# Block 0 of a latent-attention kernel: rotary scores as scaled fp16 pairs, first products in halves of tokens, values three tiles behind, loads and stores issued by SP

## The chip, the cores and the metric

The kernel runs on one core of a Trainium2 chip. The metric is the device time of one execution in microseconds, the median of several runs. A profile of one execution is read beside it: it lists the instructions of each engine (TensorE or PE with its weight loads PEld, VectorE or DVE, ScalarE or ACT, GpSimd or POOL, SyncE or SP), their waits, and the TensorE clock that was granted.

## The reference

One layer over 2048 tokens of width 512: attention with compressed queries and keys, 16 heads, a residual and a layer norm, then one linear layer with a second residual and norm.

```python
cq = rms_norm(hidden_states @ w_qa.T, q_a_ln_w)                  # 384 wide
q = (cq @ w_qb.T).reshape(b, s, H, DQ).transpose(0, 2, 1, 3)     # 128 + 64 a head
q_nope, q_pe = (q[..., :DN], q[..., DN:])
q_pe = q_pe * cos + rotate_half(q_pe) * sin
ckv = hidden_states @ w_kva.T                                    # 128 + 64
k_pe = ckv[..., KVLR:].reshape(b, s, 1, DR).transpose(0, 2, 1, 3)
k_pe = k_pe * cos + rotate_half(k_pe) * sin
ckv_l = rms_norm(ckv[..., :KVLR], kv_a_ln_w)
kv = (ckv_l @ w_kvb.T).reshape(b, s, H, DN + DV).transpose(0, 2, 1, 3)
...
scores = jnp.einsum('bhqd,bhkd->bhqk', q_full, k_full) * scale   # causal, softmax
out = jnp.einsum('bhqk,bhkd->bhqd', attn, v)
...
x = _layernorm(x + attention(x)); x = _layernorm(x + ffn(x))
```

Everything is fp32 to the reader. The kernel keeps close to fp32 by splitting most operands into a high and a low part and adding three products (high by high, high by low, low by high).

## The kernel before, in words

The 2048 tokens are four query blocks of 512 (b = 0 to 3), each block has eight pairs of heads (p) and each pair four tiles of 128 queries (qt). `units` runs over p and qt of one block. A tile of block 0 needs at most 512 keys, so both heads of a pair share one PSUM tile (`pair_scores`, L598): scores, row maximum, exponential, sums. `pair_probs` (L619) scales and splits the probabilities into two fp16 parts `hl` on ScalarE and VectorE, and SP transposes them into `PT` by DMA. `values` (L630) multiplies them with the latent keys `V`, ScalarE copies the result to `ot`, and a DMA stores it to `ot_d`. `run_values(lag)` keeps the values `lag` tiles behind the scores: 2 in block 0, up to 3 later. After block 0 all values but one tile are finished before its memory is given back.

What a score needs is made in several places:

- `project_x(hb)` (L273) takes 256 tokens: it splits x into fp32r parts (ScalarE high, VectorE low), makes the key products (`ps_kv` or `ps_x`) and the query products (`ps_cq` or `ps_x`), the inverse norms on POOL (`rsqrt`), and turns queries and keys by TensorE transposes into `cq`, `Kn` (non-rotary keys), `Kp0` (rotary keys of block 0, in fp32r, scaled by `ku`) and `Kr` (all rotary keys, unscaled). Halves 0 and 1 belong to block 0 and run first.
- `weights_q(g)` (L196) multiplies the query weights of four heads with their key weights, sums their squares for a scale (`column_total`, `root`), and splits them into fp16 pairs `wq` and `wpe`, stored to DRAM.
- `late_keys` (L372) makes the rotary keys of blocks 1 to 3 (`Kp`, fp16 pairs) once all of `Kr` is there.
- `project_pe(b, g)` (L425) makes the rotary queries of four heads: two product groups of 512 tokens, four VectorE products with cosine and sine, an add and a subtraction (POOL; VectorE for the first group), then the stack `pe`: for each of four heads the high part on partitions 0 to 63, and the low part, value less `ph`, on 64 to 127. In block 0 the high copies are ScalarE's (L462) and the low subtractions VectorE's (L465, some on POOL for the first group), in fp32r; in blocks 1 to 3 both are POOL's, in fp16.
- `project_nope(b, p)` (L471) makes the non-rotary queries `qn` of a pair as fp16 pairs.

`score` (L500) adds five products for a head: three of `qn` with `Kn`, two of the stacked `pe` with the two parts of the rotary keys. In block 0 the last two are fp32r products, for which the width is at least 256 columns (L43, L600), even in tile 0 with its 128 keys.

Halves 2 to 7 of x and the weights of groups 1 to 3 are made inside block 0: `side` holds two generators, and `units` takes steps of them after each tile (L769 to L773); `fill` takes steps of the next pair's projections.

In block 0 and before it the order of instructions on each engine is the planner's, from a simulated timeline. From block 1 on TensorE and SP keep the order of the program text. Loads of raw x, of the cosine tables for keys and of raw weights are issued on ScalarE's queue; loads of `wq`, `wpe`, `cq` and the stores of `ot` on POOL's; SP issues the first loads, the transposes and the stores of `cq`, `wq` and `wpe`.

## Time and profile before

| | |
|---|---|
| median of 3 runs | 1573.07 us (1572.97 to 1578.87) |
| the profiled execution | 1576.4 us, span 1574.5 us |
| granted TensorE clock, mean | 0.981 |
| TensorE busy | 1497.7 us, 95% |
| VectorE, ScalarE, POOL busy | 1175.2, 945.6, 364.1 us |
| first scores of block 1 | 278.5 us after the span's start |
| last scores | 1310 us after it |

A row of the timeline or of the groups names the line of the code, the operation, what is written and what is read, and the shape. `[6.28 <-DVE pe L465]` after a row is idle time of that engine just before it and what ended it. A helper that issues for several callers has one line (L74 and L75 are the fp32r split, L68 and L69 the fp16 split). TensorE rows of products that follow one another overlap; the distance between two starts is the cost of one.

### The profile page before, as it was taken

How to read it: one execution, taken by the hardware profiler on the slowest of the kernel's cores; microseconds unless marked ns; L12 is line 12 of the kernel's file. 1: busy time of each engine (PE TensorE's matmuls, PEld its weight loads, DVE VectorE, ACT ScalarE, POOL GpSimd, SP SyncE). 2: the span in 40 equal slices, each digit the busy share in tenths (PEclk: the TensorE clock that was granted, in tenths of full speed). 3: DMA queues.
4: the chain of work that ended last, by engine and by line, in shares of the span. 5: the costliest groups of instructions: out<-in, count | busy, mean ns of one | idle time of the engine just before them, and what ended most of it. 6: DMA issues, size and time to landing. Idle time of an engine off the chain costs nothing. (4 is left out here: it accounts for less than half of the span.)

```text
span 1574.5 us, 24464 instructions
## 1 busy us (share of the span) xinstructions
PE 1497.7 (95%) x9062; PEld 1007.2 (64%) x9062; DVE 1175.2 (75%) x2140; ACT 945.6 (60%) x1701; POOL 364.1 (23%) x441
## 2 busy tenths in 40 slices
PE   7799996999999999999999999999999999999997
PEld 5477764566665566666666566566566666788886
DVE  6687877788888988888887777777777775465554
ACT  5687777566666676767775665666666665311220
POOL 2232342422405504040032400400400000022132
PEclk9899998999999999999999999999999999999999
DMA  5367556587898788888896788677678898433230
GB/s 208 114 138 188 128 121 143 118 163 149 161 180 173 146 161 157 162 154 160 155 197 127 153 151 162 133 142 160 132 148 164 160 230 207 138 121 120 94 114 34
DMA packets 611142, 234.94 MB, mean 149 GB/s; under 512 B 569712, under 2 KB 589296, under 8 KB 610384
## 3 DMA queue, kind: packets, MB, share of 16 engines
q1 hardware_dynamic: 601152, 212.38, 64.0%
q0 software_dynamic: 3200, 11.44, 2.4%
q10 hardware_dynamic: 6672, 9.57, 2.1%
q8 instruction: 71, 1.16, 0.3%
q14 instruction: 47, 0.39, 0.1%
HBM read 62.72 MB, written 28.05 MB: 58 GB/s over the span
## 5 line engine op out<-in xcount | busy, mean ns | idle before, releaser
L513 PE MATMUL s<-Kn,qn 128*128 128x512 f16 (+4 forms) x1920 | 471.7, 351 | 22.4 <-ACT pr L565 17.3
L565 ACT ACTIVATE pr<-s,bias,er 128x1024 f32<-128x1024 f32 (+3 forms) x320 | 324.3, 1016 | 212.3 <-DVE bias L559 160.1
L589 DVE SCALAR_TENSOR_TENSOR hl<-pr,inv,hl 128x1024 f16<-128x1024 f32 (+7 forms) x320 | 353.5, 1118 | 42.7 <-ACT hl L586 38.0
L641 PEld LDWEIGHTS <-V 128*128 128x128 f16 x3264 | 318.6, 98 | 89.0 <-DMA PT<-hl 9.9
L641 PE MATMUL o<-ring,V 128*128 128x256 f16 x3024 | 361.5, 273 | 1.2 <-DMA ring<-hl 1.2
L513 PE MATMUL s<-Kp,pe 128*128 128x512 f16 (+6 forms) x1280 | 353.7, 358 | 7.2 <-DVE pe L465 7.2
L586 ACT ACTIVATE hl<-pr,inv 128x1024 f16<-128x1024 f32 (+7 forms) x320 | 294.2, 960 | 80.3 <-ACT pr L565 34.5
L550 DVE TENSOR_REDUCE neg<-s 128x1 f32<-128x1024 f32 (+3 forms) x320 | 317.3, 992 | 18.2 <-PE s L513 14.7
L513 PEld LDWEIGHTS <-qn 128*128 128x128 f16 x1920 | 185.8, 98 | 175.2 <-issue 36.2
L513 PEld LDWEIGHTS <-pe 128*128 128x128 f16 x1152 | 112.9, 98 | 103.4 <-issue 0.7
L482 PE MATMUL ps_qn<-cq,wq 128*128 128x512 f16 x576 | 141.5, 393 | 7.8 <-ACT ot L646 4.9
L872 PE MATMUL acc<-wvo,oh 128*128 128x512 f32 x448 | 144.4, 403 | 2.0 <-ACT pr L565 2.0
L465 POOL TENSOR_TENSOR pe<-prod,ph 32x512 f16<-32x512 f32 (+1 forms) x92 | 127.2, 1383 | 16.2 <-issue 10.3
L449 POOL TENSOR_TENSOR prod<-prod 128x512 f32<-128x512 f32 x15 | 19.1, 1275 | 467.1 <-DVE prod L442 467.1
L482 PEld LDWEIGHTS <-wq 128*128 128x128 f16 x576 | 57.8, 101 | 73.3 <-issue 15.9
L577 DVE TENSOR_SCALAR inv<-sums 128x1 f32<-128x1 f32 x128 | 27.0, 211 | 99.8 <-ACT pr L565 99.3
L872 PEld LDWEIGHTS acc<-wvo,oh 128*128 128x128 f32 x448 | 83.4, 189 | 23.3 <-issue 4.4
L872 PE MATMUL acc<-wvo,ol 128*128 128x512 f32 x224 | 87.8, 392 | 0.0
L646 ACT ACTIVATE ot<-o 128x256 f32<-128x256 f32 x128 | 48.3, 378 | 38.6 <-PE o L641 29.7
L74 ACT ACTIVATE oh<-o 128x1024 fp32r<-128x1024 f32 x28 | 29.7, 1060 | 64.9 <-PE acc L872 49.3
L464 POOL CAST pe<-prod 32x512 f16<-32x512 f32 x88 | 67.1, 763 | 3.3
L75 DVE TENSOR_TENSOR ol<-o,oh 128x1024 fp32r<-128x1024 f32 x28 | 38.9, 1390 | 38.4 <-ACT oh L74 38.4
(198 smaller groups left out, 1684.2 us busy)
## 6 DMA issues: line engine op xcount, KB each, us to landing
o<-ot_d SPq DMA_DIRECT2D x32, 512.0 KB, 3.6
ot_d<-ot SPq DMA_DIRECT2D x97, 128.0 KB, 2.4
wq<-wq_d SPq DMA_DIRECT2D x22, 384.0 KB, 3.5
wo<-in_wo_dram SPq DMA_DIRECT2D x4, 1024.0 KB, 5.7
x<-in_x_dram SPq DMA_DIRECT2D x16, 256.0 KB, 3.7
out_dram<-xb SPq DMA_DIRECT2D x16, 256.0 KB, 2.0
ot_d<-ot POOLq DMA_DIRECT2D x31, 128.0 KB, 3.4
wpe<-wpe_d SPq DMA_DIRECT2D x10, 384.0 KB, 3.8
```

The costliest lines, as they stand in the source:

```text
L75: nc.vector.tensor_tensor(l, ps, h.bitcast(F32), ALU.subtract)
L464: nc.gpsimd.tensor_copy(to, rp[q, x, :])
L465: (nc.gpsimd if not quick or (b, g) == (0, 0) and j % 2 else nc.vector).tensor_tensor(pe[64 + 32 * x : 96 + 32 * x, j, :], rp[q, x, :], ph ...
L482: nc.tensor.matmul(ps, w[:, i, lt, j * P : (j + 1) * P], cq[:, k, lt, :], start=n == 0, stop=n == 8)
L513: nc.tensor.matmul(ps[:, :w], lhs, K[:, i, c0 : c0 + w], start=n == 0, stop=n == 4)
L550: nc.vector.tensor_reduce(neg[:, ti : ti + 1], v, axis=AX.XY, op=ALU.max, negate=True)
L565: nc.scalar.activation(pr[:, c0 : c0 + n * w].rearrange("p (a c) -> p a c", a=n), v, AF.Exp, bias=bias, scale=r, accum_out=sums[:, ti : ti ...
L586: nc.scalar.activation(hl[:, 0, c], pr[:, c], AF.Copy, scale=inv)
L589: nc.vector.scalar_tensor_tensor(hl[:, 1, c], pr[:, c], inv, hl[:, 0, c], ALU.mult, ALU.subtract)
L641: nc.tensor.matmul(ps[:, :256], vt[:, i, k % 4, :], v[:, :, l, k, :], start=n == 0, stop=n == 3 * kts - 1)
L646: nc.scalar.activation(ot, ps[:, :256], AF.Copy)
L872: nc.tensor.matmul(acc, l[:, t, c], state["wvo"][p][:, i, j, :], start=p == 0 and j == 0 and n == 0, stop=p == NPAIR - 1 and j == 1 and n ...
```

## The change

Block 0's rotary keys `Kp0` become fp16 pairs. They are scaled by a factor from the squares of the rotary keys of the first 512 tokens (`key_scales(0, 4)`), where before they were fp32r pairs scaled by `ku`. The rotary queries of block 0 become fp16 pairs too, scaled by `up[0]`. Low parts are now made in one difference over all four heads (`rope_split`), and the high and low parts are then copied to their places (`rope_stack`): in block 0 the high parts by POOL and the low parts by VectorE, in the first group of block 1 both by VectorE, later both by POOL. Scores are as wide as the keys, 128 columns in tile 0.

The first products of block 0 are written out in a fixed TensorE order: keys and queries of 256 tokens, weights of group 0, keys and queries of the second 256, then rotary and non-rotary products of 256 tokens at a time, then three steps of the weights of group 1. A PSUM pool `x` of four banks serves this stage. The products of weight group 0 stay in PSUM.

In `project_x` the low part of x, the scaled `nq` and the scaled `nk` are POOL's instead of VectorE's; x is split one step ahead; a call takes two steps instead of five. The loads of x, tables and weights, and block 0's loads of `wq`, `wpe`, `cq` and its stores of `ot` are issued by SP; a store is issued after the next tile's transpose. `wq` has two buffers. Values run three tiles behind, and the last two tiles of block 0 keep their `PT` in spare room of `qn` and `pe` and are finished in block 1. Score buffers `pr` and `hl` are shared by tiles of the same parity.

```diff
-        return [[(0, max(nk, 256))]]
+        return [[(0, nk)]]
...
-    Kp0 = blk0.tile([P, 2, QB], F32R, name="Kp0")
+    Kp0 = blk0.tile([P, 2, QB], F16, name="Kp0")
...
-    def late_scales():
+    def key_scales(i, n):
...
-        nc.vector.scalar_tensor_tensor(z, fk, K_UP, kvn, ALU.mult, ALU.add)
+        nc.vector.scalar_tensor_tensor(zs[i], fk, K_UP, kvn, ALU.mult, ALU.add)
...
+        nc.vector.tensor_scalar(up[i], rz, fk, K_UP / W_TOP, ALU.mult, ALU.mult)
...
+    def raw_weights(g):
+
+        wk = pa.tile([P, 4, P], F32, tag="wk", name=f"wk{g}")
+        nc.sync.dma_start(wk, a["wk"][:, 4 * g : 4 * g + 4])
+        raws = []
+        for lt in range(LT):
+            raws.append(pa2.tile([P, 4, P], F32, tag="wqb", name=f"wqb{g}_{lt}", bufs=3))
+            nc.sync.dma_start(raws[lt], a["wqb"][g, :, lt])
+        return wk, raws
...
+    def raw_x(hb):
+
+        raws = []
+        for kt in range(0, KT, 2):
+            raws.append(pa2.tile([P, 2, 256], F32, tag="xr", name=f"xr{hb}_{kt}", bufs=2))
+            nc.sync.dma_start(raws[-1], a["xT"][hb, :, kt : kt + 2])
+        csk = pa.tile([P, 2, 2, 64], F32, tag="csk", name=f"csk{hb}", bufs=2)
+        nc.sync.dma_start(csk, a["csk"][hb])
+        return raws, csk
...
+            pin(nc.scalar.activation(h, raws[n], AF.Copy))
+            pin(eng.tensor_tensor(l, raws[n], h.bitcast(F32), ALU.subtract))
...
+        if hb < 2:
+            split16(kf, Kp0[:, 0, cols], Kp0[:, 1, cols], ks[0])
...
+            nc.gpsimd.tensor_scalar(nq, nq, rk[:, 1:2], None, ALU.mult)
...
-    state = {"queue": nc.gpsimd}
+    state = {"queue": nc.sync}
...
+    def rope_split(b, prod, ph, cols, adds, low):
+
+        rp, tp = prod[:, 0, :, cols], prod[:, 1, :, cols]
+        adds[0].tensor_tensor(rp[:, 0, :], rp[:, 0, :], rp[:, 1, :], ALU.subtract)
+        adds[1].tensor_tensor(rp[:, 1, :], tp[:, 0, :], tp[:, 1, :], ALU.add)
+        h, l = ph[:, 0, :, cols], ph[:, 1, :, cols]
+        if b:
+            nc.scalar.activation(h, rp, AF.Copy)
+            low.tensor_tensor(l, rp, h, ALU.subtract)
+        else:
+            nc.scalar.activation(h, rp, AF.Copy, scale=up[0])
+            low.scalar_tensor_tensor(l, rp, up[0], h, ALU.mult, ALU.subtract)
+
+    def rope_stack(pe, ph, cols, js, engs):
+
+        for j in js:
+            q = slice(32 * j, 32 * j + 32)
+            for i in range(2):
+                for x in range(2):
+                    r = 64 * i + 32 * x
+                    engs[i].tensor_copy(pe[r : r + 32, j, cols], ph[q, i, x, cols])
...
-        for j in range(4):
-            q = slice(32 * j, 32 * j + 32)
-            for x in range(2):
-                to = pe[32 * x : 32 * x + 32, j, :]
-                if quick:
-                    nc.scalar.activation(to, rp[q, x, :], AF.Copy)
-                else:
-                    nc.gpsimd.tensor_copy(to, rp[q, x, :])
-                (nc.gpsimd if not quick or (b, g) == (0, 0) and j % 2 else nc.vector).tensor_tensor(
-                    pe[64 + 32 * x : 96 + 32 * x, j, :], rp[q, x, :], ph[q, x, :] if b else ph[q, x, :].bitcast(F32), ALU.subtract
-                )
+        rope_split(b, prod, ph, every, (nc.gpsimd, nc.gpsimd), nc.gpsimd if b else nc.vector)
+        pe = blk.tile([P, 8 if (b, g) == (0, 3) else 4, QB], F16, tag="pe", name=f"pe{b}_{g}")
+        if b == 0:
+            engs = (nc.gpsimd, nc.vector)
+        else:
+            engs = (nc.vector, nc.vector) if (b, g) == (1, 0) else (nc.gpsimd, nc.gpsimd)
+        rope_stack(pe, ph, every, range(4), engs)
...
+        put_in()
         yield
...
+    with tc.manual_schedule(engines={ET.PE}):
...
+        keys(0)
+        nqs = queries(0)
+        x.append(split_x(1, [x_r[1][:, kt : kt + 2] for kt in (0, 2)], nc.gpsimd))
+        w0 = weights_q(0, (*wq0, wpe0, wk0, wqb_r, wpe_r))
+        next(w0)
+        keys(1)
+        turn_queries(0, nqs, "x")
+        next(w0)
+        key_scales(0, 4)
+        exp_scale(0, slice(0, 1))
+        nqs = queries(1)
+        next(w0)
+        for hb in range(2):
+            turn_k(hb, flip[hb], "x")
...
+        for hb in range(2):
+            k = "xm"[hb]
+            cols = slice(hb * 256, hb * 256 + 256)
+            for i in range(2):
+                ps = psum[k].tile([P, 512], F32, tag=k, name=f"ps_pe0_0_{i}_{hb}")
+                rope_products(wpe0, state["cq"], state["cs"], prod, ps[:, :256], i, cols)
+            rope_split(0, prod, ph, cols, (nc.vector, nc.gpsimd), nc.vector)
+            rope_stack(pe, ph, cols, range(2), (nc.gpsimd, nc.vector))
+            if hb == 0:
+                turn_queries(1, nqs, "m")
+            for j in range(2):
+                ps = psum[k].tile([P, 512], F32, tag=k, name=f"ps_qn0_0_{j}_{hb}")
+                nope_products(wq0[0], state["cq"], qn, ps[:, :256], j, cols, kvq[0])
+            rope_stack(pe, ph, cols, range(2, 4), (nc.gpsimd, nc.vector))
+            if hb == 0:
+                for _ in w0:
+                    pass
+        next_x(2)
+        state["wq", 0, 1] = wq0[1]
+        w1 = weights_q(1)
+        for _ in range(LT):
+            next(w1)
...
-        lag = min(ring.shape[1] // (2048 * (b + 1)) - 1, 3) if b else 2
+        lag = min(ring.shape[1] // (2048 * (b + 1)) - 1, 3) if b else 3
...
+                    fill()
                     pi = pair_scores(pool, b, p, qt, nk)
                     flush()
                     probs.append(pair_probs(pool, b, p, qt, nk, PT, *pi))
-                    fill()
-                    next(side[0], None)
+                    if qt != 1:
+                        next(side[0], None)
                     if p < 5:
                         next(side[1], None)
-                    if qt % 2:
-                        next(side[0], None)
+                    if p + qt == 0:
+                        next(side[1], None)
                     run_values(lag)
                     run_values(lag)
...
-    while len(vals) > 1:
+    while len(vals) > 2:
         half_values()
```

## The prediction

> **What bounds the kernel now.** The page's busy times come first, with the granted TensorE clock over forty slices.
>
> ```profile
> PE 1497.7 (95%) x9062; PEld 1007.2 (64%) x9062; DVE 1175.2 (75%) x2140; ACT 945.6 (60%) x1701; POOL 364.1 (23%) x441
> ...
> PEclk9899998999999999999999999999999999999999
> ```
>
> TensorE is busy for 95% of the span, so only its 77 us of idle time and its slow stretches can be won. Both lie at the left end. The windows view, cut where the stages change, says how much (after the name of each stretch: its length, and per engine the busy us; near the end the granted clock).
>
> ```profile
> 0.00:12.70 12.70, 8.75 (x36) 5.24 (x36) 5.69 (x19) 5.97 (x12) 2.56 (x9) 1.00 0.80 267
> 12.70:61.20 48.50, 35.15 (x202) 28.18 (x202) 33.24 (x65) 29.38 (x78) 15.63 (x27) 0.86 0.38 129
> 61.20:262.00 200.80, 184.48 (x1176) 136.79 (x1177) 160.82 (x374) 150.30 (x408) 69.62 (x119) 0.95 0.61 149
> 262.00:278.50 16.50, 6.25 (x34) 3.46 (x32) 9.92 (x18) 10.43 (x22) 2.19 (x4) 0.72 0.51 111
> 278.50:1310.00 1031.50, 1010.04 (x6455) 631.37 (x6453) 828.39 (x1462) 690.44 (x1111) 222.96 (x201) 1.00 0.80 157
> ```
>
> The rows are the wait for first inputs, the first products up to the first two score tiles, the body of block 0, its end, and blocks 1 to 3. Idle TensorE time by row: 4.0, 13.4, 16.3, 10.3 and 21.5 us, the last spread over 1031 us. A granted clock of 0.86, 0.95 and 0.72 adds about 35.15 x 0.14 = 4.9, 184.5 x 0.05 = 9.2 and 6.25 x 0.28 = 1.8 us of slowness. So block 0 after the inputs holds 40.0 + 15.9 = 56 us that are no work. Who made TensorE wait there, longest first (total, times, longest):
>
> ```profile
> PE o L641 <- DMA PT<-hl: 10.6, 3, 8.7
> PE s L513 <- DVE pe L465: 7.2, 2, 6.3
> PE ps_qt L296 <- DVE nq L354: 5.4, 2, 2.9
> PE s L513 <- ACT pr L611: 4.5, 3, 2.0
> PE ps_tot L164 <- ACT junk L219: 3.2, 1, 3.2
> PE ps_x L344 <- DVE kvr L330: 3.1, 2, 1.6
> PE ps_qn L482 <- ACT ot L646: 2.9, 1, 2.9
> ```
>
> Half of it is the rotary part (L462, L465) and what stands behind it on ScalarE. The timeline of ScalarE, VectorE, GpSimd and TensorE around the longest of the early waits:
>
> ```profile
> 50.75 1.27 ACT L462 ACTIVATE pe<-prod 32x512 fp32r<-32x512 f32 x2 [6.06 <-PE ps_wq L216]
> 55.08 5.72 DVE L465 TENSOR_TENSOR pe<-prod,ph 32x512 fp32r<-32x512 f32 x4 [2.90 <-ACT ph L453]
> 55.19 6.73 POOL L465 TENSOR_TENSOR pe<-prod,ph 32x512 fp32r<-32x512 f32 x4 [10.27 <-issue]
> 57.58 0.77 PE L513 MATMUL s<-Kp,pe 128*128 128x256 f32 x2 [6.28 <-DVE pe L465]
> ...
> 165.92 1.27 ACT L462 ACTIVATE pe<-prod 32x512 fp32r<-32x512 f32 x2
> 168.29 2.55 ACT L462 ACTIVATE pe<-prod 32x512 fp32r<-32x512 f32 x4
> ```
>
> ScalarE sat for 6.06 us before the copies because two weight loads stood ahead of them in its own queue and waited for TensorE to free their buffers. At 165.9 to 170.9 the same copies hold the eviction `ot` back, and TensorE waits 2.92 us for its PSUM.
>
> **The change part by part.**
>
> *First products (12.7 to 61.2).* TensorE's order is now fixed: rotary products come before the non-rotary ones, in halves of 256 tokens, and the weight products of group 1 stand before the scores. Its work at full clock, from start-to-start times of the timeline: two query products 4.2, weight products 2.6, two key products 2.9, four query turns 1.3, two more query products 4.4, key turns 0.9, totals 0.4, rotary and non-rotary 36 x 0.215 = 7.8, weights of group 1 2.7, four heads of scores 2.3: 29.5 us. From 12.7, where the first query product waits for its inputs, the end is at 42.2 if nothing waits; it was 61.2. The 6.3 us wait goes: the first two score tiles need only the first half of the rotary rows, and 2.0 us of non-rotary products, 4.0 us of the second half and 2.7 us of weights lie between. What is late next is ScalarE: of its 29.4 us here 5.1 (eight copies at 0.627) leave and about 1.9 (four squares of the rotary keys) come, so 26 us must fit in 30. The weight sums (six activations, about 4.7 us with their read-outs) then POOL's root and the splits stand in one chain ahead of the rotary products. I take 4.3 us of waits, from the two `nq` waits of 2.9 and 2.5 that had the same kind of chain: end at 46.5, gain 14.7. Bounds: 19.0 (no wait) and 3 (as many waits as now, 13.4, and the clock as now).
>
> *Rotary pairs.* Each of the four block-0 groups loses eight ScalarE copies (5.0 us) and eight subtractions (mean 0.788 on VectorE, 6.3 us). It gains one VectorE difference of 128x1024, near the 1.118 of the `hl` row, eight POOL copies and eight VectorE copies of 32x512 in fp16. No row has such a copy. POOL's cast of 32x512 (0.608 quiet, 1.477 at worst) is the nearest above; below, POOL's 128x64 add at 0.3. I take 0.6, 4.8 us a group on POOL. On VectorE it lies between a 128x128 fp32 multiply (0.28) and the subtraction replaced (0.684); I take 0.35, 2.8 us. So per group ScalarE -5.0, VectorE -2.4, POOL +4.8. Groups 1 to 3 are computed two tiles (13 us) before the scores that read them: two POOL adds 2.6, `ph` 1.05, the difference 1.2 and the half of POOL's copies that the first pair reads, 2.4, make 7.3 us, covered; without that cover it would cost 7.3 to 12 us a group. The price that could spoil it is in the rows above: VectorE's subtractions took 1.43 beside POOL's (5.72/4), and 0.70 at 262.8 alone (5.57/8). The Trainium skill has this as a rule in "GPSIMD Engine Reference", section "Key points": POOL shares its SBUF interfaces with VectorE and they contend. It speaks against copies on both at once; by it the copies would take twice as long and the chain 9.7 us, still under 13.
>
> *fp16 scores.* A head of 256 columns went every 0.63 us (249.96 to 250.59), of 512 every 1.17. From block 1's fp16 rows (0.81 at 384, 1.08 at 512, plus 0.055 for the mask product) they become about 0.60 and 1.135; tile 0 at 128 columns about 0.55, set by weight loads of 0.098. Over 16 heads of each of four sizes: 16 x (0.08 + 0.03 + 0.035 + 0.035) = 2.9 us. Bounds 0 and 7 (if every fp32r weight load of 0.19 had been exposed).
>
> *Work moved to POOL.* Splits of x (12 in the body, 1.28 by the 128x512 row), `nq` and `nk` (12 each, bounds 0.4 and 1.3): about 30 us on POOL, 19 off VectorE. POOL's 69.6 of 200.8 us becomes about 100 with the copies and without its DMA issues; covered.
>
> *Queues.* In the body 20 ACT loads, 31 POOL stores of `ot` and 15 POOL loads go to SP: 66 x 0.45 (SP's own issues run 0.32 to 0.59) = 30 us on a queue that now issues 32 transposes at 1.43, 46 us of 217. Behind a waiting load stand transposes, and for these the values. ScalarE loses its stops before loads; POOL loses 31 x 0.575 of issue. The lag of three tiles gives a transpose one tile more, 6.5 us (200.8/31), for the 4.7 us landing; the store of `ot` goes one tile later with two buffers, so it must land within a tile. Here a rule weighs against the move: "DMA: Bandwidth & Descriptors", section "Issuing engines are not separate DMA queues", says queues share the same DMA engines and several of them save only issue time. By it the move wins no bandwidth and costs SP those 30 us; the trace agrees that issue time is what there is.
>
> *Body.* ScalarE goes from 150 to about 130 us, VectorE from 161 to 135. The 16.3 us of idle is mostly ScalarE's lateness (4.5, 3.2, 2.9) and transposes (1.9). Nothing in the trace says what share goes: 0 to 16.3 idle, 0 to 9.2 clock. I take half of each, since small waits on `wq`, on exponentials and on new order stay: 8.2 + 4.6 + 2.5 of the fp16 = 15.3.
>
> *End.* Two values tiles instead of one pass into block 1, so the 8.7 us wait for a transpose is replaced by what block 1's first scores need: `pe` was done at 268.4 and `qn` at 270.8. TensorE waits from 267 for some 3.5 us: gain 6.5 with a little clock; bounds 0 and 12.
>
> *Blocks 1 to 3.* POOL's 16.7 us a group become one difference (about 2.5) and 16 copies at 0.6, 12 us; off the path. Nothing.
>
> Sum: 14.7 + 15.3 + 6.5 = 36.5 us. The profiled execution took 1576.4 (span 1574.5), 3.3 over the median of 1573.07; the gain is taken off the median: 1536.6.
>
> **The rivals.**
> 1. *The body keeps its waits.* VectorE is already busy 80% of it, and waits chain from exponentials to VectorE and back (ACT waits 14.9 us on `bias`, DVE 12.2 on sums). Then only start and end count: 1573.1 - 21.2 = 1552. For it: those chains; against: both engines lose a seventh.
> 2. *SP holds the transposes back a little.* 66 more issues, some waiting for buffers; 2 us lost a pair, 16 us: 1553. Against: one tile more of lag.
> 3. *Slower: SP stops.* A load whose buffer is held by POOL's split stands ahead of transposes. Three tiles are 19.5 us; less 4.7 landing and 5 of pair arithmetic, a stop under 10 us costs nothing. Above it costs its excess in each of eight pairs; it decides from 36.5/8 = 4.6 us excess, a stop of 14.6 us a pair. At 18 us: 1573.1 - 36.5 + 64 = 1601. Against: loads are prefetched a pair ahead.
> 4. *The change doesn't shorten the path.* Fixed order turns each late input into a wait: the first stage gains 3, the rest is lost to queues: about 1570.
>
> **How the numbers follow.** Forecast 0.52 (own range 1518 to 1548); rival 1 0.17, rival 2 0.13, rival 3 0.10, rival 4 0.08. All bounds at their best are 19.0 + 28.0 + 12 = 59 (1514). Leaving out rival 3, most of rival 4 and the far end of the bounds gives 1517 to 1562. Half a percent, 8 us, is about what a measurement can tell from no change. Faster by more: 0.52 + 0.17 + 0.13 and half of rival 4, 0.86; within: 0.04; slower: 0.10.
>
> **What would show it.** The wait of scores on `pe` is gone and the first exponentials start near 47 instead of 64; no ScalarE `pe` rows are left; the clock over the first 280 us is near 0.97; block 1's first scores start near 242. Wrong if: TensorE waits for `PT` grow in the body (rivals 2, 3), idle time in the body stays near 16 us (rival 1), or the first scores come after 55 (rival 4).

## The result

The changed kernel takes 1583.4 us, the kernel before 1575.0 us in the runs beside it: a ratio of 1.0051, 95% interval 1.0037 to 1.0065. The change makes the kernel half a percent slower, where 36 us of gain were forecast. All ratios here and below leave out executions in the chip's slow state, and one execution of the run `lag_two` that took 8788 us.

The page of the changed kernel, busy times and granted clock (profiled execution 1583.7 us, span 1581.9):

```profile
PE 1495.6 (95%) x9100; PEld 1004.4 (63%) x9100; DVE 1164.0 (74%) x2124; ACT 921.9 (58%) x1668; POOL 374.2 (24%) x490
...
PEclk9999999999999999999999999999999999999999
```

TensorE's work is 2 us less than before, no slice has a clock below 0.9 any more, and the span is 7.4 us longer all the same: TensorE's idle time rose from 76.8 to 86.3 us. The windows view with the cuts that the prediction used (length, then busy us of PE, PEld, DVE, ACT, POOL, then the clock):

```profile
12.70:61.20 48.50, 39.99 (x279) 34.61 (x279) 35.56 (x88) 29.05 (x91) 25.54 (x50) 0.90 0.34 117
61.20:262.00 200.80, 166.51 (x1085) 121.37 (x1084) 142.32 (x314) 125.07 (x352) 92.86 (x133) 0.94 0.59 143
262.00:278.50 16.50, 12.28 (x80) 7.38 (x78) 15.14 (x39) 9.01 (x24) 4.77 (x3) 1.00 0.56 123
278.50:1310.00 1031.50, 1007.46 (x6427) 630.01 (x6428) 823.16 (x1460) 688.00 (x1110) 195.54 (x211) 0.99 0.81 157
```

The first stage holds 4.8 us more TensorE work than before. The body holds 18.0 us less: 34.3 us of idle time instead of 16.3. ScalarE and VectorE are both less busy there than before, and GpSimd more (92.9 us against 69.6).

Three events mark the stages better than fixed cuts do: the first exponential, the first scores of block 1, the last row of scores.

| | before | after | difference |
|---|---|---|---|
| start to first exponential | 64.2 | 53.2 | -11.0 |
| from there to block 1's first scores | 214.3 | 226.9 | +12.6 |
| from there to the last row of scores | 1031.3 | 1038.5 | +7.1 |
| rest of the span | 264.6 | 263.3 | -1.3 |

So the start gained what it was meant to, block 0's body and end gave it back, and blocks 1 to 3 lost 7 us that nobody had looked for. Who made TensorE wait, in the whole changed run:

```profile
PE s L596 <- ACT pr L648: 19.8, 13, 5.3
PE s L596 <- ACT pr L694: 13.5, 7, 4.6
PE ps_qn L554 <- DVE qn L69: 7.1, 4, 2.8
PE o L725 <- DMA PT<-hl: 4.3, 1, 4.3
PE o L725 <- DVE nq L422: 3.5, 1, 3.5
PE ps_kv L316 <- DVE nq L422: 3.3, 1, 3.3
PE ps_pe L494 <- DVE nq L422: 3.3, 1, 3.3
```

The old waits (`pe`, `PT`, `ot`) are gone or shorter. New are three on the VectorE copy `nq`, four on `qn`, longer ones on the exponentials, and one of 5.3 us on an exponential of the later blocks. The timeline around one `nq` wait shows what stood ahead of it:

```profile
108.46 6.07 POOL L521 COPY pe<-ph 32x512 f16<-32x512 f16 x8 [1.25 <-ACT ph L511]
111.17 4.35 DVE L521 COPY pe<-ph 32x512 f16<-32x512 f16 x8
115.55 0.56 DVE L422 COPY nq<-ps_cq 128x384 f32<-128x384 f32 x1
116.16 1.21 PE L725 MATMUL o<-PT,V 128*128 128x256 f16 x6 [3.45 <-DVE nq L422]
```

Eight stacking copies took VectorE 4.35 us while GpSimd made its own eight. The copy that empties TensorE's PSUM buffer came behind them in VectorE's queue, and TensorE waited 3.45 us.

And where blocks 2 and 3 meet:

```profile
851.64 8.97 SPq L676 DMA_TRANSPOSE ring<-hl  x2
...
862.50 1.20 ACT L648 ACTIVATE pr<-s,bias,er 128x1024 f32<-128x1024 f32 x1 [5.72 <-DMA ring<-hl]
863.85 0.96 PE L596 MATMUL s<-Kn,qn 128*128 128x320 f16 x3 [5.33 <-ACT pr L648]
```

An exponential waits here for a transpose, although it reads nothing that the transpose writes. It waits for memory that the transpose still reads.

### The profile page after: what moved, and what is told of

It reads as the page before. It is cut to its first block, busy times and chain, and to the rows that moved or that the text cites. A ratio compares the mean times of both kernels' runs of the same rounds, so it can differ in the third digit from the quotient of the medians.

```text
span 1581.9 us, 24566 instructions
## 1 busy us (share of the span) xinstructions
PE 1495.6 (95%) x9100; PEld 1004.4 (63%) x9100; DVE 1164.0 (74%) x2124; ACT 921.9 (58%) x1668; POOL 374.2 (24%) x490
## 5 line engine op out<-in xcount | busy, mean ns | idle before, releaser
L596 PE MATMUL s<-Kn,qn 128*128 128x512 f16 (+5 forms) x1920 | 467.4, 350 | 37.9 <-ACT pr L648 19.8
L596 PE MATMUL s<-Kp,pe 128*128 128x512 f16 (+5 forms) x1280 | 342.7, 350 | 1.2 <-DVE pe L521 1.2
L596 PEld LDWEIGHTS <-pe 128*128 128x128 f16 x1280 | 125.2, 99 | 108.9 <-POOL pe L521 1.4
L521 POOL COPY pe<-ph 32x512 f16<-32x512 f16 (+1 forms) x216 | 162.0, 750 | 22.1 <-ACT ph L511 6.9
L554 PE MATMUL ps_qn<-cq,wq 128*128 128x512 f16 (+1 forms) x594 | 139.6, 382 | 8.4 <-DVE qn L69 7.1
L494 PE MATMUL ps_pe<-cq,wpe 128*128 128x512 f16 (+1 forms) x306 | 69.8, 376 | 5.3 <-DVE nq L422 3.3
```

What stands on the lines that cost most here:

```text
L494: nc.tensor.matmul(ps, w[:, i, lt, x * P : (x + 1) * P], cq[:, k, lt, cols], start=n == 0, stop=n == 3 * LT - 1)
L521: engs[i].tensor_copy(pe[r : r + 32, j, cols], ph[q, i, x, cols])
L554: nc.tensor.matmul(ps, w[:, i, lt, j * P : (j + 1) * P], cq[:, k, lt, cols], start=n == 0, stop=n == 3 * LT - 1)
L596: nc.tensor.matmul(ps[:, :w], lhs, K[:, i, c0 : c0 + w], start=n == 0, stop=n == 4)
```

## The experiments

Theory A, from the traces: GpSimd's new work is what costs. Its copies slow VectorE's copies, and what TensorE waits for stands behind them in VectorE's queue. Theory F: the wait where blocks 2 and 3 meet comes from buffer addresses. Rivals: SP's single queue and the buffers that two query tiles share (B), the new order of projection step and scores (C), the rows moved to GpSimd by their own length (D). Each run is compared with the kernel before on its own chip, so ratios are what to compare; 0.001 is 1.6 us. Two executions of the same block 0 differ by about 3 us.

### Where blocks 2 and 3 meet

Block 3's two pools are laid over the memory that block 2's pools gave back. As the programs place them, the first exponentials of block 3 occupy bytes 16,384 to 24,576 of a partition of that region. The last transpose of block 2 reads the fp16 buffer at 12,288 to 18,432 in the changed kernel and the one at 6,144 to 12,288 in the kernel before. With the pools in the other order these exponentials occupy bytes 0 to 8,192. Both runs make the same edit, in one kernel each; it takes the last transpose's buffer out of their memory in the changed kernel and puts it there in the kernel before.

```diff
-                pools = [... for k in ("hl", "pr")]
+                pools = {k: ... for k in (("pr", "hl") if b == 3 else ("hl", "pr"))}
+                pools = [pools["hl"], pools["pr"]]
```

> The changed kernel with one edit: block 3's two pools are allocated in the other order, so that the memory of its first exponentials is no longer the memory of the last transposed fp16 buffer of block 2. Theory F (buffer placement costs the 5.3 us wait at 863.85, where blocks 2 and 3 meet): that TensorE wait falls from 5.33 to about 1 us, block 3 starts some 4.5 us earlier, and the time is about 1583.4 - 4.5 = 1579. Rival (the wait is the transposes' lateness from the SP queue, whatever memory they write to): the wait stays at 4 to 5 us at the same place, and the time stays at 1583. Block 0 must stay as it is in both: first scores of block 1 at 280 +- 1.

> The kernel before with the same edit of block 3's pools, which in that kernel puts the first exponentials of block 3 onto the memory of the last transposed buffer of block 2, as the changed kernel has it. Theory F: a TensorE wait of 4 to 5 us appears where blocks 2 and 3 meet (0.69 us at 855.88 before), and the time is about 1575.0 + 4.5 = 1579.5. Rival (SP queue of the changed kernel): no new wait, 1575.

Measured: 0.9992 (0.9977 to 1.0008) for the changed kernel with the edit, 1.0036 (1.0018 to 1.0053) for the kernel before with it. The exponential in question, first in the changed kernel with the edit:

```profile
854.01 1.21 ACT L648 ACTIVATE pr<-s,bias,er 128x1024 f32<-128x1024 f32 x1 [0.41 <-DMA ring<-hl]
```

Then the scores in the kernel before as it was, and the exponential and the scores in it with the edit:

```profile
855.88 0.57 PE L513 MATMUL s<-Kn,qn 128*128 128x320 f16 x3 [0.69 <-ACT pr L565]
```

```profile
858.32 1.20 ACT L565 ACTIVATE pr<-s,bias,er 128x1024 f32<-128x1024 f32 x1 [6.39 <-DMA ring<-hl]
859.67 0.96 PE L513 MATMUL s<-Kn,qn 128*128 128x320 f16 x3 [6.00 <-ACT pr L565]
```

The wait goes with the overlap in both directions: 5.3 us vanish in one kernel, 5.3 appear in the other (0.69 to 6.00). From block 1's first scores to the last row of scores the changed kernel needs 1032.3 us with the edit, near the 1031.3 before. Theory F holds, for 5.7 us by the ratio of the second run and 6.2 by the stages of the first. The first run's total fell by 9 us; the rest lies in block 0, where both kernels have the same program (first scores of block 1 at 276.9 instead of 280.1), so it is put down to the spread between executions. The rival, transposes that are late because of SP, falls: the kernel before does not have the new queue and shows the wait.

### The stacking copies

First the high halves from GpSimd to ScalarE:

```diff
-                    engs[i].tensor_copy(pe[r : r + 32, j, cols], ph[q, i, x, cols])
+                    (ScalarE: activation Copy; VectorE: tensor_copy)
-            engs = (nc.gpsimd, nc.vector)
+            engs = (nc.scalar, nc.vector)
...
-            engs = (nc.vector, nc.vector) if (b, g) == (1, 0) else (nc.gpsimd, nc.gpsimd)
+            engs = (nc.scalar, nc.vector) if (b, g) == (1, 0) else (nc.gpsimd, nc.gpsimd)
```

The second pair of lines belongs to the same edit: ScalarE also takes the high halves of block 1's first group, which the change has on VectorE. The halves in the first products (32x256) stay where they were, here and in all later runs.

> The changed kernel with the high halves of block 0's rotary stacking copies (8 per group) on ScalarE instead of GpSimd; VectorE keeps the low halves. Theory A (VectorE's fp16 copies take 0.55 us instead of 0.30 because GpSimd copies at the same time, and nq and qn stand behind them in VectorE's queue): VectorE's 8 copies fall from 4.4 to about 2.4 us a group, the TensorE waits on nq at 116 and 189 (3.45 and 3.29 us) and on qn at 59 (2.76) lose 1 to 2 us each, idle TensorE time in 46.5 to 262 falls from 38.6 to about 30, and block 1's first scores come near 273 instead of 280. ScalarE has 5 us more a group, which may take back 1 to 2 us a group. Rival B (SP's queue and shared buffers): VectorE's copies get shorter, but idle time stays within 3 us of 38.6 and block 1's scores within 2 us of 280.

Then all sixteen to GpSimd:

```diff
-            engs = (nc.gpsimd, nc.vector)
+            engs = (nc.gpsimd, nc.gpsimd)
```

> The changed kernel with all 16 stacking copies of groups 1 to 3 of block 0 on GpSimd, none on VectorE. Theory A: VectorE has no row of these copies in the body, nq never stands behind them, the waits on nq at 116 and 189 go, idle TensorE time in 46.5 to 262 falls by 6 to 10 us, unless the copies, 16 x 0.6 = 9.6 us in a row on GpSimd, end later than the scores that read them (then a wait of scores on pe of up to 3 us a group takes the place). Block 1's first scores near 273 to 277 instead of 280. Rival D (work moved to GpSimd is what is late): GpSimd has 5 us more a group, its nk, nq and split rows come later, and idle time rises by 3 to 5 us a group, scores near 290.

Measured: 0.9991 (0.9979 to 1.0002) with ScalarE, 1.0053 (1.0031 to 1.0075) with all on GpSimd. ScalarE's case came out as theory A had it: block 1's first scores at 270.7 instead of 280.1, and the same place in the timeline reads

```profile
108.50 5.11 ACT L522 ACTIVATE pe<-ph 32x512 f16<-32x512 f16 x8
110.03 2.41 DVE L524 COPY pe<-ph 32x512 f16<-32x512 f16 x8
115.49 0.55 DVE L422 COPY nq<-ps_cq 128x384 f32<-128x384 f32 x1
```

Eight VectorE copies take 2.41 us instead of 4.35 when GpSimd makes none beside them. At this very place next to nothing is won. `nq` comes at 115.49 where it came at 115.55, because `kvr`, ahead of it in VectorE's queue, now waits for a ScalarE row behind ScalarE's copies, and TensorE waits 3.20 us for `kvr`:

```profile
114.16 0.42 DVE L326 COPY kvr<-ps_kv 128x256 f32<-128x256 f32 x1 [1.72 <-ACT junk L324]
114.64 0.59 PE L165 MATMUL ps_tot<-wsum,ones 128*128 128x6 f32 x2 [3.20 <-DVE kvr L326]
```

The gain comes later in the body: over all of it the waits on `nq` fall from 10.4 to 0.7 us. The price is ScalarE's 5.1 us a group: at 182.8 TensorE waited 5.66 us for an `ot` eviction behind them (and behind the weight rows that follow them), the kind of wait that the kernel before had there.

The other run is a miss of theory A as I had put it. The waits on `nq` at 116 and 189 went, but the total did not improve; the copies of a group took GpSimd 11.3 to 12.8 us (0.70 each in the mean), and waits on transposes rose to 12.6 us in 5. Taking the copies out of VectorE's queue was not enough. Taking them off GpSimd helped, here and in the next runs.

The same two questions, now with block 3's pools in the other order, and with all sixteen copies on VectorE as the sharper test:

```diff
(act_swap: the edits of stack_act and swap_after; dve_swap: that of swap_after and)
-            engs = (nc.gpsimd, nc.vector)
+            engs = (nc.vector, nc.vector)
```

> The changed kernel with both edits that helped: the high halves of the stacking copies on ScalarE, and block 3's pools in the other order. If theories A and F are separate causes their gains add: block 1's first scores near 271 (as with the copies alone), the wait where blocks 2 and 3 meet near 1 us instead of 5.3, and a time of about 1574.0 - 6 = 1568, ratio to before 0.995 (faster than both kernels). If they are one cause seen twice, 1573 to 1574.

> The changed kernel with block 3's pools in the other order and all 16 stacking copies of a group of block 0 on VectorE, none on GpSimd. Theory A (the two engines slow each other's copies): VectorE makes twice as many copies in about the same time, 16 x 0.30 = 4.8 us a group instead of 8 x 0.55 = 4.4, GpSimd loses 5.6 us a group, the waits on nq stay within 1 us, and the time is that of the kernel with the pools' order alone, 1574 to 1576. Rival (a copy of 32x512 costs VectorE 0.55 us whatever GpSimd does): 16 x 0.55 = 8.8 us a group, 4.4 more than now in front of nq and qn, block 1's first scores at 285 or later, time 1585.

Measured: 0.9955 (0.9939 to 0.9971) and 0.9925 (0.9899 to 0.9950). The gains of A and F add, with F at the 0.0036 of the kernel before (1.0051 - 0.0060 - 0.0036 = 0.9955). With all sixteen copies VectorE is done in 2.35 + 2.68 = 5.0 us a group, 0.7 us more than it needed for eight, and the kernel is 0.007 faster than with the pools' order alone. So GpSimd's eight copies brought nothing: they nearly doubled the price of VectorE's.

### The rows moved to GpSimd

The low part of raw x, and the scaling of `nq` and `nk`, back on VectorE; first with the copies on ScalarE, then with the copies as the change has them, then with all copies on VectorE too. Block 3's pools are in the other order in all three.

```diff
-            xsplit[hb] = split_x(hb, raws, nc.gpsimd), csk
+            xsplit[hb] = split_x(hb, raws, nc.vector), csk
-            nc.gpsimd.tensor_scalar(nq, nq, rk[:, 1:2], None, ALU.mult)
+            nc.vector.tensor_scalar(nq, nq, rk[:, 1:2], None, ALU.mult)
-        nc.gpsimd.tensor_scalar(nk, kvr[:, :P], rk, None, ALU.mult)
+        (nc.gpsimd if hb < 2 else nc.vector).tensor_scalar(nk, kvr[:, :P], rk, None, ALU.mult)
```

> The kernel of the run with both edits, with the low part of the raw x and the scaling of nq and nk back on VectorE (about 19 us in the body), as in the kernel before. Rival D (GpSimd's longer rows, nq 1.30 and nk 0.64, set the wait): the waits that name nq lose 1 us each and the body gets 2 to 4 us shorter. Theory A (VectorE's queue is what is late): its work in the body rises from 158 to about 175 us of 215, and block 1's first scores come 2 to 6 us later than 271.

> The changed kernel with block 3's pools in the other order and the low part of raw x, nq and nk back on VectorE; the stacking copies stay as the change has them, eight on GpSimd and eight on VectorE a group. Theory A' (each piece of work on GpSimd costs: it is itself two to three times as long there, and it stretches VectorE's own rows): the gain of the moved rows, 12 us, comes here too, 1574.5 - 12 = 1562.5, and VectorE's copies beside GpSimd's stay near 0.5 us. Rival (the rows were only late because the copies shared the engine with them): half the gain or less, 1568 to 1573.

> The changed kernel with block 3's pools in the other order, and raw x, nq, nk and all 16 stacking copies on VectorE. Theory A' (GpSimd's share is what costs; VectorE has room as long as it is not slowed): 1563.9 - 12 = 1552, V's row back at 0.28 us, the copies near 0.30. Rival (VectorE, some 175 us of the body's 203, becomes the bound): 1560 to 1566, with TensorE's waits on VectorE rows growing past 12 us in the body.

Measured: 0.9887 (0.9855 to 0.9919), 0.9953 (0.9936 to 0.9969) and 0.9922 (0.9907 to 0.9937). The first is a miss of theory A as it was put, and a hit of D in its direction, larger in size: I expected VectorE, with 17 us more to do, to be later, and the kernel got 0.007 (11 us) faster (0.006 by a second run of the same kernel, below). The windows from the first exponential to block 1's first scores, one for each kernel (length, busy PE, PEld, DVE, ACT, POOL). The kernel before:

```profile
64.20:278.54 214.34, 190.77 (x1209) 140.25 (x1209) 168.28 (x387) 159.44 (x426) 71.10 (x122) 0.93 0.61 148
```

The changed kernel:

```profile
53.17:280.11 226.94, 184.08 (x1186) 131.47 (x1187) 165.75 (x371) 136.93 (x388) 102.14 (x144) 0.93 0.57 136
```

Copies on ScalarE (act_swap), and then x, `nq` and `nk` on VectorE as well (dve_back):

```profile
53.44:269.64 216.20, 181.34 (x1186) 129.66 (x1187) 157.63 (x364) 158.72 (x424) 85.43 (x120) 0.95 0.58 143
```

```profile
53.13:258.80 205.67, 178.36 (x1186) 128.94 (x1187) 161.26 (x400) 157.62 (x424) 46.59 (x84) 0.96 0.61 150
```

These four lines carry the case. The change took rows worth some 26 us off VectorE by the prediction's count, and VectorE's busy time in block 0 fell by 2.5 us. Giving 16.9 us of them back (12 x 0.684 for x, 12 x 0.422 for `nq`, 12 x 0.306 for `nk`) raised it by 3.6 us only. On GpSimd the same rows had taken 39 us (12 x 1.32, 12 x 1.30, 12 x 0.64), and while they ran VectorE's other rows were longer.

With the copies still on both engines (dve_split) the gain was 0.004 instead of 0.007, and two waits of 3.5 and 3.3 us on `nq` were still there. With everything on VectorE (dve_everything) it was nothing beyond dve_swap. The stretches from the first exponential to block 1's first scores, in us, put the runs side by side (two numbers are two runs):

| | copies on GpSimd and VectorE | on ScalarE and VectorE | all on VectorE |
|---|---|---|---|
| x, `nq`, `nk` on GpSimd | 226.9, 224.0 | 216.2, 216.2 | 204.5 |
| x, `nq`, `nk` on VectorE | 219.2 | 205.7, 209.4 | 205.0 |

So the moved rows cost some 5 to 10 us of block 0, or nothing where all copies are on VectorE, although `V` took 0.443 us there too. Longer rows on VectorE are not enough to make the kernel late. What the runs with all copies on VectorE lose against dve_back comes behind the stretch, in the first 20 us of block 1 (length, then busy TensorE): dve_swap, dve_everything, dve_back.

```profile
258.46:278.46 20.00, 14.48 (x76) 7.54 (x74) 15.60 (x36) 10.84 (x22) 4.05 (x3) 0.91 0.51 111
257.89:277.89 20.00, 13.23 (x65) 6.58 (x63) 15.84 (x39) 6.95 (x14) 1.56 (x2) 0.83 0.48 81
258.80:278.80 20.00, 20.00 (x106) 11.02 (x105) 16.06 (x33) 10.87 (x19) 4.67 (x3) 0.90 0.65 125
```

TensorE idles there for 5.5 and 6.8 us, all but a little of it in waits of 1.2 to 2.7 us on rows of VectorE, which in these two runs also makes all sixteen copies of block 1's first group. In dve_back ScalarE has half of them.

One thing these runs leave open. In block 0 the order on each engine is the planner's, and an edit of GpSimd's, ScalarE's or VectorE's work changes it. Of the 1443 TensorE rows from 12.7 to block 1 in the run with the pools' order alone, all stand in the order of the changed kernel; of the 1444 with the copies on ScalarE some 1090 do. What of a gain is the edit and what is the new order, these runs do not part.

Is it the length of GpSimd's own rows in the chain, or GpSimd's activity as such? In the next run the kernel dve_back keeps all results as they are, and GpSimd does idle arithmetic of the same size at the same places:

```diff
+    dm = pa.tile([P, 256], F32, tag="dm", name="dm")         # all of it in halves 2 to 7 only
+                for _ in range(2):                       # in split_x
+                    nc.gpsimd.tensor_tensor(dm, dm, dm, ALU.subtract)
+        nc.gpsimd.tensor_scalar(dm[:, :P], dm[:, :P], 1.0, None, ALU.mult)      # beside nk
+            for w in (256, 128):                         # beside nq
+                nc.gpsimd.tensor_scalar(dm[:, :w], dm[:, :w], 1.0, None, ALU.mult)
```

> The kernel of the run dve_back, where GpSimd in addition does idle arithmetic of the same size at the places where the changed kernel gives it raw x, nq and nk (two subtractions of 128x256, scalings of 128x256 and 128x128, and one of 128x128, all on a tile of its own that nobody reads). Theory A' by contention (GpSimd's activity stretches VectorE's rows and delays GpSimd's own later rows): V's row goes from 0.28 towards 0.40, VectorE's work in the body rises by 5 us or more, and half or more of the 12 us come back: 1563 to 1569. Rival (what cost was only the chain through GpSimd: nq and nk take 1.30 and 0.64 us there and TensorE's turns wait for them): nothing reads the idle work, so 1557 to 1560.

Measured: 0.9934 (0.9915 to 0.9953), against 0.9887 and, in a second run of the same base further below, 0.9898 (0.9883 to 0.9913). By these ratios idle work of 43.8 us cost 5.7 to 7.4 us, half or more of the 9 to 11; the interval overlaps with that of the first base and lies just clear of the second's. The stretch from the first exponential to block 1's first scores took 211.0 us against 205.7 and 209.4. Groups of VectorE rows in block 0, without the idle work (the second run of the base), then with it (busy us, mean ns of one, idle before):

```profile
L524 DVE COPY pe<-ph 32x512 f16<-32x512 f16 x32 | 9.4, 295 | 0.6
L422 DVE COPY nq<-ps_cq 128x384 f32<-128x384 f32 x12 | 6.6, 550 | 5.3 <-ACT junk L353 5.2
L701 DVE TENSOR_SCALAR inv<-sums 128x2 f32<-128x2 f32 x30 | 5.0, 167 | 14.0 <-ACT pr L697 13.8
L344 DVE SCALAR_TENSOR_TENSOR V<-nk,V 128x128 f16<-128x128 f32 x12 | 3.4, 281 | 0.4 <-ACT V L343 0.4
```

```profile
L533 DVE COPY pe<-ph 32x512 f16<-32x512 f16 x32 | 10.8, 338 | 0.5
L429 DVE COPY nq<-ps_cq 128x384 f32<-128x384 f32 x12 | 6.6, 547 | 4.8 <-ACT junk L360 4.7
L710 DVE TENSOR_SCALAR inv<-sums 128x2 f32<-128x2 f32 x30 | 8.2, 272 | 9.7 <-ACT pr L706 9.6
L351 DVE SCALAR_TENSOR_TENSOR V<-nk,V 128x128 f16<-128x128 f32 x12 | 4.9, 411 | 0.8 <-ACT V L350 0.8
```

Several kinds of rows that read and write SBUF got longer although nothing reads the idle work: `pe`, `inv` and `V` above, the scaling `nk` (0.299 to 0.365) and others. Not all did: the `Kp` difference stayed at 0.744 and 0.746, and the median of all `hl` differences at 0.608 and 0.607. No row that reads PSUM got longer. VectorE's busy time in the stretch rose by 7 us (161.3 and 160.7 to 168.3). That GpSimd's activity lengthens VectorE's rows is therefore shown. That it costs the kernel time is likely, for about half of the gain. The idle work also delays GpSimd's own real rows in its queue and changes the planner's order (some 1270 of 1440 TensorE rows keep theirs), and this run cannot part these. The other half is left to the longer chain through GpSimd, by exclusion, which was not shown.

### The queues

The edit puts the queues back, on the kernel act_swap; then only the stores of `ot` and the loads of `wq`, `wpe`, `cq` and block 1's table, on the kernel dve_back (block 0's table stays on SP in both).

```diff
-    state = {"queue": nc.sync}
+    state = {"queue": nc.gpsimd}
-            nc.sync.dma_start(raws[-1], a["xT"][hb, :, kt : kt + 2])     # queue_back only:
+            nc.scalar.dma_start(raws[-1], a["xT"][hb, :, kt : kt + 2])   # x, tables, weights
```

> The kernel of the run with both edits (copies on ScalarE, block 3's pools), with the loads of raw x, tables and group weights back on ScalarE's queue, and the stores of ot and the loads of wq, wpe and the queries' tables back on GpSimd's queue in block 0. Rival B (SP's one queue delays transposes): waits of the values on transposes in block 0 fall from 9.5 us (4 times) to under 5, block 1's first scores come 4 us or more earlier than 271. Theory A alone (SP's queue was covered): ScalarE's stops before loads come back, no gain or up to 5 us lost.

> The kernel of the run dve_back (copies on ScalarE, the moved rows on VectorE, block 3's pools in the other order), with only the stores of ot and the loads of wq, wpe and the queries' tables back on GpSimd's queue in block 0; SP keeps the loads of x and weights, so that the start stays as it is (first exponential at 53). Rival B in what is left of it (in the run with both queues back the stretch from the first exponential to block 1's scores was 209 us against 216): waits of the values on transposes fall from 9.0 us to 5, block 1's first scores come 3 to 5 us before 258.8, 1557.4 - 4 = 1553. SP's queue covered: 1557 +- 2.

Measured: 1.0018 (0.9991 to 1.0045) against 0.9955 for its base, and 0.9932 (0.9909 to 0.9955) against 0.9887 and 0.9898. Both moves back cost by these ratios: the first 10 us (8 without one execution of 1593.7), the second 5 to 7, with intervals that overlap with its base's. With the loads on ScalarE's queue the first exponential is late again, by 9 us:

```profile
62.40 0.46 ACT L697 ACTIVATE pr<-s,bias,er 128x128 f32<-128x128 f32 x1 [5.18 <-DVE bias L693]
```

Waits on transposes fell in the first run, as rival B had it (8.2 to 5.3 us), and did not matter. So SP's queue is a good part of the change, mostly by the start. One more reading: that run began its exponentials 9.0 us later than its base, reached block 1's scores 1.9 us later and stood idle for 3.9 us in the 30 us after 270, where its base did not. Some 3 of the 9 us were made up on the way, so a gain at the start need not be kept whole (the run also moved the stores' queue).

### Order, buffers and lag

On the kernel dve_back, which was run again as the base on the same chip, one edit each:

```diff
(fill_after: fill() below pair_probs again, as in the kernel before)
(own_hl)
-        hl = pool.tile([P, 2, 2, nk], F16, tag=f"hl{qt % 2}", ...)
+        hl = pool.tile([P, 2, 2, nk], F16, tag=f"hl{qt}", ...)      # cqst: bufs=1
(lag_two)
-        lag = min(ring.shape[1] // (2048 * (b + 1)) - 1, 3) if b else 3
+        lag = min(ring.shape[1] // (2048 * (b + 1)) - 1, 3) if b else 2
```

> The same kernel as the run dve_back (copies on ScalarE, x, nq and nk on VectorE, block 3's pools in the other order), as the base for the runs beside it: 1557 +- 3, block 1's first scores at 259 +- 2.

> The kernel of the run dve_back with one edit: in block 0 the projection's step (fill) is written after a tile's scores and probabilities again, as in the kernel before, instead of ahead of its scores. Rival C (with the step ahead, scores of two tiles stand close together and TensorE waits for the exponentials that hold the scores' PSUM, 9.3 us in 5 waits): these waits fall to under 5 us as before (4.5), and block 1's first scores come 3 to 5 us earlier than 259, total 1553. If the order is free: +-1.5 us.

> The kernel of the run dve_back with one edit: each of the four query tiles of block 0 has its own fp16 buffer again (the change lets tiles 0 and 2, and 1 and 3, share one); the key turn's staging has one buffer for that. Rival B (a transpose that stands in SP's queue behind a load holds the buffer, and ScalarE's next fp16 copy waits for it: PT waits of TensorE 9.0 us in 4, ScalarE's hl waits 2.6 in 3): ScalarE's waits on transposes go, TensorE's waits on PT fall to 5 us or less, 3 to 4 us earlier. If the sharing is covered: +-1.5 us; the single staging buffer could cost up to 2 us.

> The kernel of the run dve_back with one edit: block 0's values run two tiles behind the scores again instead of three. If the third tile is what covers SP's queue, the waits on transposes grow from 9.0 us by 2 us in most pairs, 10 us or more, total 1567. If two tiles cover as well, +-2 us, and the end of block 0 carries one tile less: its wait for the last transposes may fall from 4.0 to 2 us.

Measured: base 0.9898 (0.9883 to 0.9913); the old order 0.9881 (0.9865 to 0.9898); own buffers 0.9885 (0.9870 to 0.9900); a lag of two 0.9949 (0.9932 to 0.9966). The third tile of lag is worth 8 us in all: without it block 1's first scores come at 268.5 instead of 261.7. Of these 6.8 us 3.0 lie before the first exponential (55.3 instead of 52.3), where no values stand yet, and come with the planner's other order; 3.8 lie behind it. The mechanism was not the expected one, since waits on transposes did not grow (5.6 us in 3). The waits went to `kvr`, `nq` and `qn` instead (4.0, 4.0 and 4.3 us, once each), presumably because the older tile's values no longer stood ahead of them as work for TensorE; that was not tested. Order and own buffers gained 2.7 and 2.0 us by these ratios, inside overlapping intervals. The waits on block 0's exponentials did fall with the old order, from 9.4 to 4.7 us, while waits on transposes rose from 6.9 to 11.0. With own buffers ScalarE's waits for transposes went (3.2 us to none), TensorE's did not (7.1).

### All that helped together, and the end of block 0

```diff
(combined: dve_back with the edits of fill_after and own_hl; carry_three: that and)
-    while len(vals) > 2:
+    while len(vals) > 3:
```

> All edits that helped, together: copies' high halves on ScalarE, x, nq and nk on VectorE, block 3's pools in the other order, the projection's step after the scores, an fp16 buffer for each query tile. If the last two gains (2.7 and 2.5 us against their base of 1559.1) add: 1559.1 - 5 = 1554. If both only shift the same slack: 1556. Body idle of TensorE from 46.5 to 250 falls from 24 to 20 us if they add.

> The kernel of the run combined, where block 0 carries three tiles of values into block 1 instead of two, so that no values stand between block 0's last scores and its end. If the wait for the last transposes (4 us or more at 258) is what is left of the end, it moves behind block 1's first scores and 2 to 4 us are won: 1551. If block 1's first scores themselves come late (their rotary copies and qn), nothing or less than 1 us.

Measured: 0.9882 (0.9861 to 0.9904) and 0.9871 (0.9856 to 0.9886). The two small gains are not seen to add; their sum, 0.9868, would still lie in the interval. The last TensorE row of block 0 that waits, in combined and then in carry_three:

```profile
258.00 1.46 PE L728 MATMUL o<-PT,V 128*128 128x256 f16 x6 [5.84 <-DMA PT<-hl]
```

```profile
259.41 0.49 PE L728 MATMUL o<-PT,V 128*128 128x256 f16 x3 [2.69 <-DMA PT<-hl]
```

With three tiles carried, block 1's first scores go ahead of it (252.6 instead of 259.3) and half of the wait is filled; the total falls by 0.0011, which these intervals do not separate from nothing. The kernel carry_three, 1554.2 us beside 1574.9 for the kernel before, beats both kernels, by 1.3% and 1.8%.

## Why the prediction was wrong

**First products** (gain 14.7): right in kind. The 6.3 us wait on `pe` is gone, so are the ScalarE copies, and the first exponential came 11.0 us earlier. It came at 53.2 and not at 47. The rows of the first score tile show where the 6 us went:

```profile
44.35 0.28 PE L596 MATMUL s<-Kn,qn 128*128 128x128 f16 x2
47.54 0.22 PE L596 MATMUL s<-Kp,pe 128*128 128x128 f16 x1
50.49 0.22 PE L596 MATMUL s<-Kp,pe 128*128 128x128 f16 x1
50.74 0.43 DVE L688 TENSOR_REDUCE neg<-s 128x2 f32<-128x256 f32 x1 [1.31 <-PE s L596]
52.46 0.36 DVE L690 TENSOR_SCALAR bias<-neg,er 128x2 f32<-128x2 f32 x1
53.17 0.45 ACT L694 ACTIVATE pr<-s,bias,er 128x128 f32<-128x128 f32 x1
```

TensorE had the first head's scores from 44.0 to 44.3, but the second head's two rotary products stood behind products of group 1's weights and of the next `qn`. The row maximum needs both heads. The bias then stood behind a difference `ph` in VectorE's queue, which waited for ScalarE. ScalarE itself, which the step named as late next, held the exponential back for the last 0.4 us only. The step had all four heads of scores done by 46.5; their order on TensorE, which the fixed list no longer covers, was not in its sum. By its own terms the lower bound of 3 us should also have been about 1.

**Rotary pairs** (covered, so a price of nothing): the step that failed first, and the costliest. With the high copies on ScalarE the stretch was 8 to 11 us shorter, with all on VectorE 20 us. Its sizes were low, 0.35 us for a VectorE copy (0.567 in the mean) and 0.6 for a GpSimd copy (0.706), and the VectorE difference took 1.42 instead of 1.2. The error of reasoning is another: I asked whether the chain would be done before the scores that read it, and it was (one wait of 1.2 us on `pe`). I did not ask what stands behind 4.4 us of copies in VectorE's queue, which is `nq` and `qn`, and with them TensorE's PSUM. The prediction had the contention in its own rows, VectorE's subtractions at 1.43 us beside GpSimd's and 0.70 alone, and used it only for the covered chain.

**Work moved to GpSimd** (covered, 30 us there and 19 off VectorE): mis-sized, 39 and 16.9 us, and not covered where other copies load ScalarE or GpSimd. With this and the rotary step VectorE was to go from 161 to 135 us in the body. Over the whole stretch of block 0 it went from 168.3 to 165.8. The rows were two to three times as long on GpSimd, the top of the bounds I had given for `nq`, and they stretched what was left on VectorE. Undoing the copies and the moved rows together brings 0.010 (0.9992 to 0.9887 or 0.9898), some 15 to 17 us.

**Body** (15.3, half of the idle time and half of the clock's slowness): nothing in the trace supported the half, as the step said itself. Idle time doubled instead, and over the first 280 us the clock was 0.94 (0.92 before) and not 0.97. ScalarE's relief did arrive (159 to 137 us) and bought nothing in the changed kernel. When it was given its copies back and VectorE its rows, TensorE was idle for 27.3 us of the stretch instead of 42.9 (205.67 - 178.36 and 226.94 - 184.08): an engine's busy share did not tell how late its rows would be here.

**Queues** and the lag: right in effect. In the changed kernel no values waited for a transpose before the end of block 0, so rivals 2 and 3 fall, and going back costs 5 to 10 us. (In dve_back, where the rest is quicker, such waits are 9.0 us.) That the third tile is needed was right by 8 us, but not for the reason given: it was to cover the transposes, and without it the waits on them did not grow. That part was luck.

**fp16 scores** (2.9): right for 384 and 512 columns (a head every 0.86 and 1.13 us), too small for 128, where the next head starts after 0.34 us (44.01 to 44.35) and not after 0.55. With 16 heads of each size that makes the gain about 6 us, an estimate from these spacings.

**End** (6.5): the 8.7 us wait for a transpose became one of 4.3 us, and a wait of 2 to 6 us for the last transposes stayed in most of the runs. What I had put in its place, block 1's `pe` and `qn`, came last only with all copies on VectorE (`pe`, by 1.4 us, and `qn`, by 1.3).

**Blocks 1 to 3** (nothing): 7.1 us lost, of them 5.3 at the one wait on memory. No line of the diff touches this place; the order in which buffers come free there did change.

Of the rivals, the fourth (the start gains, the rest is lost, about 1570) was nearest, though the start gained 11 us and not 3, and the loss had another cause than the queues it named; the one that ended slower named SP and was false. No rival had GpSimd as the culprit. None of the three signs of being wrong came either: the first scores were in time, no wait on `PT` grew in the body, and idle time there did not stay near 16 us but doubled. And that half of the early waits were the rotary part counts every wait on ScalarE with it; its own rows, `pe` and `ot`, are 10.1 of the 36.9 us listed. What stays open: even in the best kernels without a third carried tile block 0 needs 204 to 209 us from the first exponential to block 1's scores, where the forecast had 214.3 - 21.8 = 192.5. Waits of 1 to 6 us on `nq`, `kvr`, exponentials and transposes are left there, and no single one of them was shown to be the cause. The planner's order, new with every edit, is the rival that no run tests.

## What to carry to other kernels

Moving work to GpSimd is not free because GpSimd is idle: price it by its effect on VectorE's rows beside it, and by whatever stands behind the longer rows in VectorE's queue, PSUM evictions first. Ask of every added group not only who reads it, but who queues behind it. And when a change far away lengthens a later block by one wait, look at whether two buffers share memory there: an exponential that waits for a transpose that it does not read is the sign, and laying out the pools in another order is the test.

## What the hardware showed

VectorE's 32x512 fp16 copy from SBUF to SBUF took 0.295 us in the mean with GpSimd quiet, 0.338 beside the idle work, 0.567 where GpSimd made copies of the same kind. Single copies show more. In the changed kernel, one of each engine in the middle of the group shown above, and VectorE's last one, after GpSimd had finished:

```profile
111.98 0.60 POOL L521 COPY pe<-ph 32x512 f16<-32x512 f16 x1
112.10 0.63 DVE L521 COPY pe<-ph 32x512 f16<-32x512 f16 x1
115.23 0.29 DVE L521 COPY pe<-ph 32x512 f16<-32x512 f16 x1
```

And a copy of GpSimd in the run where VectorE made none:

```profile
114.10 0.61 POOL L521 COPY pe<-ph 32x512 f16<-32x512 f16 x1
```

While both copied, one copy of each engine started every 0.65 us (GpSimd at 111.98, 112.63 and 113.27, VectorE at 112.10, 112.75 and 113.39). GpSimd alone went at the same 0.65. So GpSimd kept its pace, and VectorE, which needs 0.29 alone, was held to it. Other rows beside the idle work: the 128x128 difference `V` went from 0.28 to 0.41 us, the tiny 128x2 row `inv` from 0.167 to 0.272. Rows that read PSUM did not change: `nq` 0.550 and 0.547.

The Trainium skill says in "SBUF — State Buffer", section "SBUF: two separate sides", that VectorE in some forms of its instructions and GpSimd share one port pair, which one of them holds for a whole instruction while the other is fully blocked. That only rows without PSUM were stretched agrees with it. The size does not look like a full block: taking turns by whole instructions, a copy of each engine would need 0.60 + 0.29 = 0.89 us, an estimate from the rows above, and the pair took 0.65. "Perfetto Trace Analysis", section "Optimizing Scalar/DVE Operations", adds that offloading between these two might not help because of that port. In this case it cost: 0.004 to 0.007 of the time for the copies, and for the moved rows 0.007, 0.004 or nothing, by where the copies were.
